# Transposed adjacency in blocks, and new order tables, in a four-layer graph network kernel

## The chip, the cores and the metric

One core of a Trainium2 chip runs the whole program in one launch. The metric is the device time of that launch in microseconds (us). The engines are TensorE (PE, with its weight loads as PEld), VectorE (DVE), ScalarE (ACT), GpSimd (POOL) and SyncE (SP, which here only issues transfers).

## What is computed

32 graphs ("batches"), each with 512 nodes of 128 features and a 512 x 512 matrix of zeros and ones in which about 3% are ones. Four residual layers, each on the row-normalised and rectified input:

```python
h = relu(layernorm(x)); x = x + L0(h)   # edge convolution: max over neighbours
#   p = h @ (W1 - W2); q = h @ W2; L0[n] = max_j relu(p[n] + q[j] + b) * adj[n, j]
h = relu(layernorm(x)); x = x + L1(h)   # 4 sublayers: adj_rownorm @ src, adj_colnorm.T @ dst, self; tanh
h = relu(layernorm(x)); x = x + L2(h)   # (adj / rowsum) @ (h @ w2) + b2
h = relu(layernorm(x)); x = x + L3(h)   # 4 steps of a gated unit (GRU) on adj.T @ (h @ w)
```

## The kernel before

**How it is staged.** `batch` (L1875) records all work of one graph: `load`, `prepare` (layer 0: layer norm, both copies of the adjacency, the neighbour lists), `gathers` (layer 0: the maximum over neighbours), `layer1`, and `layer23` (layers 2 and 3). A node takes its maximum over neighbours in two ways: up to 7 neighbours come as rows gathered by indirect transfers that POOL issues (`G<-qtab,idx`, folded in by DVE as `gm<-gm,G`), and the rest by products with one-hot matrices (`oh<-ccd` on DVE, `pa<-oh,qhl` on PE, folded in by DVE as `acc<-acc,pa`).

**Who sets the order.** Nothing is issued while it is recorded. `Flow` (L804) takes the operations of all batches and issues them one by one (`Flow.run`, `step`), engine by engine in the order of due times, which stand as text in tables: one row for each of the three weight preparations and each of the first and last batches (`FRONT`, `BACK`), and one row `MIDDLE` that is used for all batches between them, shifted by `PERIOD`. The same pass keeps a small model of engines, the port that DVE and POOL share, and the transfers; it decides ties, which PSUM bank an operation gets, and where filler matmuls (`spin`, L1077) go: they are put in front of a PE operation that the model sees start late. So the model and the tables change the program only through the order on each engine, the choice of buffers and the fillers. About four batches are under way at once: while the GRU steps of one batch run, another is in `layer1`, and two later ones are in `gathers` and `prepare`.

**The parts that matter below.**

- The transposed adjacency: four `ab` tiles (bf16 copies of 128 rows each, by ACT) go through four transposing transfers on SP into one tile `abt` (L1530 to L1532). ACT then casts it into `at`, with four operations that each read one quarter of the columns of all four transfers (L1533 to L1536). `View.meets` (L654) decides for `Flow` whether two operations touch the same part of a tile; it looks at partitions and at the second dimension of the tile alone.
- A layer norm (`norm`, L1439): DVE makes the mean and variance, then `rstd` and `shift` in small operations; POOL raises `rstd` to the power -1/2 (`rstd<-rstd,mhalf`, 128x4) and multiplies `shift` (`shift<-shift,rstd`); ACT applies both (`xn`). For layers 1 to 3 the result is split in a high part (ACT, `hi`) and a low part (POOL, `lo<-xn,hi`).
- A GRU step in `layer23`: ACT makes two gates from `pk`, POOL makes `zc = 1 - z` (`zc<-gate`), DVE multiplies `gate<-h,gate` and `nn<-nn,zc` and adds them to `h<-gate,nn`, and PE transposes `h` (`ph<-ident,h`). The transposes, and all of the next step, wait for that `h`.
- All recorded operations carry line L1051 in the profile.

Of the kernel before, what the change touches and what calls it, by code (L numbers as in the profile page):

```python
# [15 lines left out]
BF16 = mybir.dt.bfloat16  # L16
# [3 lines left out]
AF = mybir.ActivationFunctionType  # L20
# [5 lines left out]
P = 128  # L26
# [12 lines left out]
PERIOD = 80.8143  # L39
# [3 lines left out]
    380.50,  # L43
    (
        "!!!!4>!)u!,w!*U!*A!,i!3b!-/!,p!7K!Cx!Ux!f?!|6!{j!zs!{@!m&!Ac!kD##:#%##YH#[H#[S#bg#gz!ob!"
        "zw#$+#*u#eY#fJ#g:#hO#k~#o[#pD#q2#o/#ld#qT#u]#r%#rf#tq#w5#r%#n]#oE#pe#rR#p(#s3#p+#ve$$X#w"
        "G#x($#;#uc#x0$,&#z+$+F$*)#we#}S$%9$,d$*f$#x#iW#r_$.<$2A$=j$>/$C7#@0#w|#|j#}C#}U#~2#~{#x&"
        "#x.#y/#y6#yQ#z=#y=#yD#{K#{i#|[#}G#|W#}+#}=$(s$,F$.R$.H$I3$/I$CT$E!$EA$/w$1=$4)$6n$2c$=$$"
        "5K$@w$84$Am$:&$CC$>P$H{$A^$Ix$D-$No$H+$Ra$Il$T7$M)$U4$OW$[n$TC$`;$Uf$az$W,$aJ$]W$eb$`t$l"
        "&$c+$ko$ea$nT$gg$p*$l`$tk$n%$yS$oH%!S$sj$}S$u_$}j#{(#|@#~h$$%$&e#{z$*_$-&$+w$/R$#3$.3$0q"  # L50
        "$2?$4|$&&$3@$5i$6G$7c$1Q$6`$8N$;[$=v$47$<n$>b$=*$?N$6s$?W$@:$?p$A/$<C$BB$D9$C`$E$$Bb$F.$"
        "FY$Go$H>$CW$I$$Kt$LS$Ox$Eb$Nx$SV$OU$Vs$I;$Ye$]d$]l$_%$Ru$^($b2$_k$bz$V5$bb$cf$cz$dR$^D$d"
        "d$h!$fM$k2$ev$j}$l<$lc$q~$x4$yA$z!$zj%#4%$R%&s%&S%)F%(6$Jy%*5$b,%%t%>L$fe%Gk%H)%1z%47%0y"
        "%1n%0^%5I%5B%2d%8L%94%9z%:*%A9%B~%BC%AM%Aw%CW%DD%QZ%HR%Kq%M8%Pg%Q*%IW%Ip%J+%Jq%K+%L8%LO%"
        "M[%NG%JY%KB%KY%K|%L}%Ms%Qt%Rt%SC%W;%Wj%Xe%Y`%Zn%[f%[q%]B%]M%]m%^X%_8%_g%_~%`9%a9%bi%c#%d"
        "$%dO%_O%`~%b!%b:%c;%cR%cj%dS%e0%aP%dj%ee%f`%gn%iS%it%j!%j.%jL%k?%k{%lM%le%mN%r)%r@%rW%ro"
        "%sY%l6%l|%m7%m|%n7%qV%qn%s*%t:%mf%nN%oI%pD%sm%u(%v-%w<%x;%xM%xj%y&%zu%|M%}H&$i&%#&%R&&;&"
        "&j&($&(S&.{&$P&%j&&$&(<&)%&)=&)T&*&&-k&(k&/4&3M&5C&6=&7P&8z&:!&@l&BP&C_&Dv&E$&E0&E:&Ei&L"
        "r&K@&Hn&FU&M8&MF&M*&M?&N6&NN&N.&O[&RA&O~&QK&Qu&Rx&Si&_h&Y%&Yu&Z_&Zv&[<&[T&[k&^U&ct&et&fr"
        "&g+&gL&hp&kG&hU&lA&jE&kw&l[&lp&k@&l:&m:&m3&mS&mt&mL&o$&o9&oc&q.&pa&vD&w0&u(&u:&uE&uP&uo&"  # L60
        "w(&w~&xy&y5&yK&yc&yz&z5&zd&z{&{I&|H&}B&}V&~Q(!C&{M&~D&~C(!R(#?(#3($0(&2((,((7((B((M((l()"
        "Z((X()R(*M(*f(*}(+8(+O(+}(,8(,O(,{(.t(-y(0%(0a(2_(0A(26(2V(3H(45(40(5%(6`(7c(8i(8s(9Q(9p"
        "(;K(9](:V(;Q(=B(=Y(=q(>,(>C(?m(@((@R(AQ(C4(B`(Do(Ea(<$(D9(DW(E{(Fh(Fp(GX(HM(Ig(Iq(I|(J+("
        "JJ(K<(J6(K1(L,(LN(Lg(L~(M8(Mg(M~(N9(Ne(Oc(Ph(Q?(Q{(Rx(Nh(Qc(R,(Rz(Sg(S[(TW(UM(Vf(W,(W7(W"
        "X(X-(XG(Xv(Z*(ZP"
# [4 lines left out]
        1.64,  # L70
        (
            "!!!!!&!1Y!2%!1n!2E!2p!%3!4:"
# [3 lines left out]
        1.24,  # L76
        (
            "!+N!3i!4n!0#!.N!5,!4&!6]!75!6w!8]!8B!95!7O!8w!7j!9O!/9!8(!>p!?2!?R!3L!A_!Aw!@a!C{!A=!AT!"
            "AG!Aj!&7!!!!>{!BN!C$!Ck!)_!C;!CY!D0!Jb!4A!D]!E*!E]!F@!F-!F.!Fp!NO!HN!N;!NZ!,a!?=!FY!G(!G"
            "Z!H>!CY!J&!JP!K&!L2!E*!KS!K}!LS!R@!M#!M$!MP!N4!QY!O$!Y!!GT!G(!O:!OE!Q>!R8!Ra!S.!JP!RU!Rw"  # L80
            "!SJ!T+!TW!U+!K}!TL!TA!Tk!V0!WC!Wm!VQ!VR!W-!{,!Yj!~q#!q!N4!Od!XX!V~!Xd!YC!ed!]N![m!f6!k$!"
            "xR!x^!xG!yp!z]!zr!{O#.0!mW!{e!{D!{p!|f!}Q!}h!~9!~d!~O!~P!~f#$$##J##m#$0"
# [3 lines left out]
        7.83,  # L86
        (
            "!&R!(=!zB#$+##|#$6#$z#&@!!!#$Y#%)#%?#&r!,%#$e#$o#%4#(<#))#*?#()#/d#18#/o#2}#&X#0L#0)#/z#"
            "2E#32#4?#2b#=+#<|#=V#=v#0k#=6#=A#=K#?N#@;#A3#>w#F(#F`#F3#Gg#>J#F>#FI#FT#Fs#G`#I&!)(#H]#J"
            "r"  # L90
# [5 lines left out]
            "!!!!!M!!!!)I!)x!)^!)5!)q!*>!*0!*7!*X!*q!*P!,9!,M!,w!-C!-m!.D!.C!7@!:?!@N!-0!-Y!.&!.O!/&!"  # L96
            "1;!:?!@A!F/!Lo!M`!NP!Os!3T!4{!6.!Of!4#!4O!5i!:U!8#!6]!8r!9i!6]!NM!Q9!RX!Te!Qx!UE!N}!R;!X"
            "a!V%!Vc!X#!OO!R}!^i!WC!^,!]K!Pr!ZK![.!`*!_I![k!S*!SK!U=!U_!Us!V+!_?!S;!Q.!Q5!RH!R{!UJ!WR"
            "!R$!R,!R3!R:!S6!T!!RA!RO!RV!R^!Tj!V+!SR!SY!S`!Sg!Vr!X=!Y(!YH!Y>!VG!aK!iq![8!^;!f#!`O!ar!"
            "d^!c8!gF!q3!kZ!hi!j8!l}!v|!nC!q,!rN!of!~a!vY!sq!{L!u7#(=!w~##5!~T#$Z#.n#%}#(n#+p#*7#4*!Z"  # L100
            "C![>!]/![V!]s![h!]d!^_!^5!_J!Z|!]`!_.!`7!_E!a!!^|!a[!c*!cT!cA!dA!b%!cX!e-!cp!eu!bc!d+!fb"
            "!dB!gM!bx!d7!eb!h9!ey!i%!eS!g-!hV!k%!ho!kn!ic!j^!lY!k0!mF!jD!k_!n2!l1!nz!hH!ie!l`!og!m2!"
            "pR!k$!l@!mk!s3!n=!s{!qp!rl!th!s&!uS!rQ!sM!v?!se!w]!m]!q$!s{!xI!t6!{`!rA!va!x/!|K!xF!}8##"
            "=##H##S##_#4s#65#9J#7Y#9i#7y#:A!YX!]<!_P!Z9!ti!u&!rB#<V#=*#<B#<k#=W#=I#=!#=P#=j#C9#=q#DF"
            "#Q4#Ot#O##P@#Qk#S=#!Z#Qs#Q~#R]#Rg#W$#Rr#Tp#T}#U9#UF#Ux#V4#VM#Vn#T=#UR#Ul#V(#VA#VY#Vs#W!#"
            "WC#U-#Vf#W/#W;#WH#WT#Wa#Wz#Xw#U_#Wn#X*#X6#XC#Xh#Xu#Y$#YE#XO#X[#Y1#Z,#Y]#ZW#[A#[&#[S#]J#]"
            "!#]I#^*#^B#^>#^h#^b#_/#^v#_G#_S#_a#_m#`)#`N#`t#a8#_-#_y#`6#`B#`Z#`h#a##ac#b^#a1#a=#aI#aU"
            "#ao#a{#b+#bP#c##b8#bD#b]#bj#bv#c%#c3#c?#dL#cK#cW#ce#d4#d`#e2#er#e^#fn#gQ#fP#f[#h0#h;#g.#"
            "gW#hZ#i(#hF#hy#i)#iB#iZ#j0#j=#jI#k]#hS#h`#i5#iN#ih#it#jU#jb#k%#hm#j##jo#j{#k+#k7#kD#ld#m"
            "(#kP#k]#kj#l%#l2#l?#lK#lW#nI#kv#ob#lq#oo#m@#p>#ml#pj#n;#q9#ng#o6#pR#qe#r4#rt#rx#s2#sS#tK"  # L110
            "#sP#sz#u/#uX#t,#tn#t{#u+#ut#v8#vE#vQ#z6#t?#u7#uD#uP#ug#v^#vj#vw#xd#w&#w3#w@#wL#wX#we#wr#"
            "x9#|l#xE#xQ#xk#y&#y4#yK#yd#yq#{,#x_$!F#z,$!R#zW$!~#{&$#M#{R$#y#|9$$H#|f$%0#}5$%[#~3#~_$#"
            "6$&+$&V$(:$(m$(x$)%$)]$0z$2O$3k$2d$2;$2x$5[$3&$4t$5z$6@$6c$7M$9h$:4$:^$7b$;8$<=$??$<m$=p"
            "$>,$>C$>f$>}$?8$@<$@h$H4$HJ$H`$IG$J1$L!$JK$MX$L=$LP$Kk$M~$Le$Lp$NQ$NJ$Nk$PI$Nd$QV$S.$R7$"
            "Ra$Qk$VC$W/$T)$T4$T?$Ud$Wv$Xw$Yr$Zm$[($[?$[n$])$]@$]W$]o$^=$_<$`U$`J$ad$bU$^A$aP$a7$b_$c"
            "K$c?$d<$eY$fN$fY$fe$fp$g2$i$$fz$i+$jU$jm$k>$kU$km$l($lV$ln$m=$o6$n;$pD$q#$rM$p1$q+$q_$rP"
            "$s=$s1$t.$uL$vA$vd$w+$w6$wT$z<$wA$yN$zH${~$|9$|P$}!$}:$~K$~{%!I%#H%$f%$V%%u%&g$zx%&H%%D%"
            "(q%)^%)f%*Z%+^%,^%,i%,t%-!%-B%.1%-.%.)%/!%/R%/u%00%0G%0v%11%1H%1s%2r%3l%4$%4{%8:%1w%5m%4"
            "n%6{%7h%8y%9Y%:E%;:%;^%<#%</%=i%>&%<X%>~%?H"
# [3 lines left out]
        3.50,  # L123
        (
            "!!!!>B!.:!.q!.N!.%!.c!/4!/)!.j!/F!/_!/M!0l!<2!=(!<Z!?T!Mg!L6!MY!V3!]2!SU!Sv!T;!TF!Tf!PE!"
            "VD!]j!g2!pR!qC!r3!s#!U]!VB!XI!X&!Vn!Xq!YS!^c!y#!x?!zx!|X!_0!u`!v/!wN!y-!vn!yj!v<!wj!}.!x"
            "L!{m!~K!x[!yd#&u!|M#&8!}k!{Q#$8#%W#(U#)6#$w!ta!yS!~<#%u#(>#(R#4Y!a?!|O!|l!|z!}$#&T#(@!|V"
            "!|^!|e!|s!}_#![!},!}3!}9!~%#$}#%j!}m!}t!}{!~-#*T#,X#-W#;[#.W#+4#7U#99#:y#<?#=b#?(#/*#C)#"
            "4z#D[#6@#F.#8v#Gl#Co#L~#E8#N`#Fq#Qb#HN#RW#MZ#Uf#O<#WF#RK#ZU#Sn#]4#VA#_L#X0#a;#[2#d<#]m#f"
            "L#`)#hK#as#jM#eR#m]#g)#o3#i&#tS#k)#tr#n9#vD#ol#ww!~z#!v#&[##a#)+##F#%)#)s#*+#-i##*#$j#.S"  # L130
            "#/!#.l#/k#(1#)L#/&#38#/=#4##0L#1[#4l#2B#5X#2V#4z#6D#5A#70#-w#0j#5g#7y#6S#8e#2*#3E#8]#:{#"
            "8u#=%#;d#<_#=o#<v#>Z#<D#=@#?F#=W#@3#5>#:3#=}#@{#>i#Ag#=G#>c#@1#C{#@H#Dp#BG#Ef#FB#E}#G/#C"
            "=#FO#H##Fg#K3#@!#C*#F~#K|#G=#M6#D_#FL#H*#N!#O0#P6#Q*#Q5#QM#QX#xP#yo#{8#{v#|9#{V#|k#9z#2U"
            "#18#1u$&!$&=#z@#~[#~3#~p#~G$!e$#S$!l$#Z$#n$&Z$#u$(h$*?$)r$)I$(|$,P$.#$+w$*~$+X$,7$,Y$-)$"
            "-x$/V$/n$0)$0@$1A$2+$2X$3($.;$0o$1*$1p$2A$3+$3B$3Y$4)$3q$4,$5&$6h$8p$9f$:C$:N$;^$;|$<_$<"
            "m$=Y$=q$>,$>r$?D$?s$A.$AY$=($>Z$?[$@.$@[$@s$AE$A]$B:$?-$At$CA$D<$EJ$F?$Fa$Fl$Fw$G9$Gx$H*"
            "$Ik$L:$LP$N=$NS$Nk$O%$Pl$HA$J&$J=$Jl$K~$Mj$N%$OD$Ov$HX$Hp$K&$Lo$Oj$Ql$S/$T=$U2$UD$UO$Up$"
            "V2$Xu$Z-$_M$_}$`O$`g$a8$ag$bP$iN$]9$`}$aO$a~$b9$bh$c:$g)$h1$c!$dx$j,$o)$p#$q6$rH$uV$zT$|"
            "9$}G$~^%!d%!o%!z%#B%&I%)A%%T%$`%+%%+-%*t%*{%+q%,-%,0%-:%/u%/K%..%-a%0N%3x%0b%8H%9=%9T%9l"
            "%:&%:>%:U%<@%B^%D/%DD%DZ%D|%FC%I,%F(%Im%H0%IR%J2%JF%If%J+%JZ%Jf%Jy%K4%K#%LG%M)%L[%M{%MQ%"  # L140
# [2221 lines left out]
```

## Time and profile before

| what | value |
|---|---|
| median of 3 runs (lowest to highest) | 2829.79 us (2827.24 to 2830.96) |
| profiled execution, device time | 2828.67 us |
| its span, first to last instruction | 2827.0 us |
| mean granted TensorE clock | 0.991 |
| PE busy | 2723.7 us, 96% |
| DVE busy | 2432.8 us, 86% |
| POOL busy | 1730.0 us, 61% |
| ACT busy | 1268.1 us, 45% |

A busy PE is not a PE at its peak: the end of a matmul in the profile includes the time until its result stands, so two matmuls in a row overlap in the listing, and a short wait of PE can hide inside "busy". The useful number is the distance between the starts of two matmuls.

### The profile page before, as it was taken

Reading aid. Unit: us, or ns where it says so; the run is one execution under the profiler, and the core shown is the slowest. Engines: PE = TensorE matmul, PEld = TensorE weight load, DVE = VectorE, ACT = ScalarE, POOL = GpSimd, SP = SyncE. Lnnn points to the kernel's source line nnn. Section 1 sums busy time; section 2 is a strip of 40 time slices with the busy share of each in tenths; the row PEclk is TensorE's granted clock in tenths of the full one; section 3 lists DMA queues with packets and bytes.
Section 4 is the critical chain, followed back from the end, with each engine's and each line's share of the span. In section 5 each row is a group of like instructions: output and inputs, shape, how many; then the busy total and the mean of one; then the engine's idle time right before and its main releaser. Section 6 shows DMA issues by size and latency. Waiting matters only on the chain.

```text
span 2827.0 us, 36274 instructions
## 1 busy us (share of the span) xinstructions
PE 2723.7 (96%) x10703; PEld 1719.5 (61%) x10718; DVE 2432.8 (86%) x5739; ACT 1268.1 (45%) x2623; POOL 1730.0 (61%) x1892
## 2 busy tenths in 40 slices
PE   7799999999999999999999999999999999999997
PEld 3475656666666665666666666666656666556575
DVE  6888988999999998999999999999989998888543
ACT  6644444444444443444444444454444444434333
POOL 4666565666666676666667666666766666765311
PEclk9899999999999999999999999999999999999998
DMA  7754443444444443444444445444444444433100
GB/s 165 126 89 86 91 88 72 84 83 85 98 94 93 73 86 79 86 98 93 91 70 84 86 87 98 93 93 72 84 83 86 94 95 87 69 65 57 32 4 9
DMA packets 256752, 233.81 MB, mean 83 GB/s; under 512 B 98426, under 2 KB 205092, under 8 KB 256548
## 3 DMA queue, kind: packets, MB, share of 16 engines
q0 software_dynamic: 47104, 92.34, 24.3%
q1 hardware_dynamic: 143172, 81.41, 11.7%
q10 hardware_dynamic: 66272, 57.68, 6.7%
q8 instruction: 87, 1.43, 0.2%
q14 instruction: 117, 0.96, 0.1%
HBM read 163.79 MB, written 17.17 MB: 64 GB/s over the span
## 4 chain that ended last, share of the span: by engine, by line
PE 79%; DVE 10%; POOL 4%; issue 4%; ACT 3%; DMA 1%; SPq 0%; DVEq 0%; ACTq 0%; POOLq 0%
PE pg L1051 24%; PE pu L1051 18%; PE pk L1051 13%; PE pa L1051 6%; PE phn L1051 3%; PE pxn L1051 3%; PE ph L1051 2%; DVE nn L1051 2%; DVE acc L1051 2%; PE pq L1051 2%; PE pf L1051 1%; POOL G L1051 1%; PE pt L1051 1%; PE po L1051 1%; PE pkey L1051 1%
## 5 line engine op out<-in xcount | busy, mean ns | idle before, releaser
L1051 POOL DMA_INDIRECT G<-qtab,idx x744 | 829.3, 1115 | 380.6 <-DVE gm L1051 172.7
L1051 DVE TENSOR_TENSOR acc<-acc,pa 128x512 f32<-128x512 f32 x992 | 673.8, 679 | 63.3 <-PE pa L1051 30.3
L1051 PE MATMUL pa<-oh,qhl 128*128 128x512 f32 x1024 | 482.3, 497 | 15.9 <-issue 6.3
L1051 PE MATMUL pg<-an,hi 128*128 128x512 f32 (+1 forms) x1072 | 464.1, 439 | 4.4 <-ACT hi L1051 3.7
L1051 PE MATMUL pu<-ag,w 128*128 128x512 f32 (+1 forms) x952 | 443.7, 571 | 0.0
L1051 PE MATMUL pg<-an,lo 128*128 128x512 f32 (+1 forms) x1072 | 413.4, 392 | 0.0
L1051 DVE TENSOR_SCALAR oh<-ccd 128x1024 fp32r<-128x1024 bf16 x492 | 344.8, 703 | 7.1 <-DMA ccd<-cc 3.8
L1051 ACT ACTIVATE xn<-x,shift,rstd 128x128 f32<-128x128 f32 x512 | 219.3, 486 | 208.3 <-POOL shift L1051 195.0
L1051 PE MATMUL pg<-at,hi 128*128 128x512 f32 (+1 forms) x672 | 272.6, 415 | 1.1 <-ACT hi L1051 0.8
L1051 PEld LDWEIGHTS pa<-oh,qhl 128*128 128x128 f32 x1024 | 191.5, 190 | 129.3 <-issue 66.3
L1051 PE MATMUL pg<-at,lo 128*128 128x512 f32 (+1 forms) x672 | 265.3, 398 | 1.5 <-POOL lo L1051 1.3
L1051 PE MATMUL pk<-mT,g_ih 128*128 128x512 f32 (+1 forms) x528 | 252.2, 586 | 4.6 <-ACT mT L1051 4.1
L1051 PEld LDWEIGHTS pg<-an,hi 128*128 128x128 f32 x1072 | 202.1, 189 | 86.0 <-issue 36.6
L1051 ACT ACTIVATE gate<-pk,bsum 128x512 f32<-128x512 f32 (+1 forms) x264 | 171.7, 673 | 170.2 <-PE pk L1051 133.8
L1051 PE MATMUL pk<-h,g_hh 128*128 128x512 f32 (+1 forms) x528 | 245.1, 586 | 0.6 <-ACT h L1051 0.5
L1051 PEld LDWEIGHTS pu<-ag,w 128*128 128x128 f32 x952 | 172.4, 191 | 118.8 <-issue 81.9
L1051 PEld LDWEIGHTS pg<-an,lo 128*128 128x128 f32 x1072 | 201.9, 188 | 65.3 <-issue 17.5
L1051 POOL TENSOR_TENSOR rstd<-rstd,mhalf 128x4 f32<-128x4 f32 x128 | 162.4, 1269 | 114.7 <-DVE rstd L1051 89.0
L1051 DVE TENSOR_TENSOR ag<-pg,rbc 128x512 f32<-128x512 f32 (+1 forms) x272 | 172.3, 652 | 53.0 <-PE pg L1051 42.7
L1051 DVE TENSOR_TENSOR gm<-gm,G 128x128 f32<-128x128 f32 x744 | 215.1, 296 | 0.2
L1051 POOL TENSOR_TENSOR lo<-xn,hi 128x512 fp32r<-128x512 f32 x96 | 123.2, 1283 | 139.4 <-ACT hi L1051 138.6
L1051 ACT COPY mT<-pg 128x512 f32<-128x512 f32 (+1 forms) x164 | 93.7, 571 | 206.4 <-PE pg L1051 178.6
(178 smaller groups left out, 5132.2 us busy)
## 6 DMA issues: line engine op xcount, KB each, us to landing
ccd<-cc SPq DMA_DIRECT2D x512, 64.0 KB
an<-in_adj_dram POOLq DMA_DIRECT2D x128, 256.0 KB
af<-in_adj_dram ACTq DMA_DIRECT2D x31, 1024.0 KB
rbc<-scal SPq DMA_DIRECT2D x32, 512.0 KB
x<-in_x_dram ACTq DMA_DIRECT2D x62, 256.0 KB
G<-qtab,idx POOLq DMA_INDIRECT x744
qtab<-qn SPq DMA_DIRECT2D x32, 256.0 KB
out_dram<-xo ACTq DMA_DIRECT2D x32, 256.0 KB
```

What stands on the lines that cost most here:

```text
L1051: op.fn(*(real(v) for v in op.args), **{k: real(v) for k, v in op.kw.items()})
```

## The change

1. `abt` gets a fourth dimension. Transfer `it` now writes the block `abt[:, it, :, :]`, and ACT's cast reads `abt[:, :, jt, :]`, four pieces of 128 elements, and writes the same 512 elements of `at` as before. Seen by `View.meets`, the four transfers now touch different parts of the tile.
2. The model in `Flow`: a gather takes 0.55 instead of 0.35 of the shared transfer time; `idx` counts as ready 0.3 later; and a POOL operation that is not itself on the shared port (kind 1: such as `rstd`, `shift`, `g`, `dinv`) is placed behind a DVE operation that uses the port, when that one starts within `LOOK` = 0.1 after it.
3. All order tables are new. `FRONT` has 12 rows instead of 10, so that `MIDDLE` stands for 13 batches instead of 15. `PERIOD` is 80.7843 instead of 80.8143.

No other operation is added, removed or resized: the program has the same operations on every engine, apart from the filler matmuls (181 instead of 209) and the waits that follow from the order.

```diff
-PERIOD = 80.8143
+PERIOD = 80.7843
...
     HOLD = 0.6
+    LOOK = 0.1
...
         elif "pool" in at and ops["pool"].kind in (1, 2):
             at["pool"] = max(at["pool"], self.port["vec"] - self.YIELD)
+            near = self.LOOK if ops["pool"].kind == 1 else 0.0
+            if "vec" in at and ops["vec"].port and at["pool"] <= at["vec"] < at["pool"] + near:
+                at["pool"] = at["vec"] + 1e-6
...
-                self.shared = shared + (0.35 if op.after > 5.0 else 1.38)
+                self.shared = shared + (0.55 if op.after > 5.0 else 1.38)
...
-        abt = F.tile(big, [P, NT, N], BF16, tag="abt", name=f"abt_{b}")
+        abt = F.tile(big, [P, NT, NT, P], BF16, tag="abt", name=f"abt_{b}")
         for it in range(NT):
-            F.sync.dma_start_transpose(out=abt[:, :, it * P : (it + 1) * P], in_=abs_[it])
+            F.sync.dma_start_transpose(out=abt[:, it, :, :], in_=abs_[it])
         for jt in range(NT):
             F.act.activation(
-                at[:, jt, :], abt[:, jt, :], AF.Identity, accum_out=deg[:, 1, jt : jt + 1]
+                at[:, jt, :].rearrange("p (i q) -> p i q", q=P), abt[:, :, jt, :], AF.Identity,
+                accum_out=deg[:, 1, jt : jt + 1],
             )
...
             idx, at8[:, :, 0 : left(b)], float(N), none[:, :, 0 : left(b)], ALU.min, ALU.max
         )
+        F.part[-1].after += 0.3
```

The rest of the diff is the text of the tables.

## The prediction

> **What bounds the kernel now.** I read the busy time of the engines by stretches first, then the chain that ended last in order of time, then the timeline of one middle batch, and last the lists of waits. The stretches (each about one batch; columns: PE, PEld, DVE, ACT and POOL busy, clock, DMA share, GB/s):
>
> ```profile
> 302.00:383.00 81.00, 79.61 (x308) 49.63 (x307) 74.41 (x167) 36.35 (x76) 48.68 (x53) 1.00 0.44 79
> 1595.00:1676.00 81.00, 80.67 (x314) 50.66 (x311) 74.35 (x175) 36.59 (x78) 53.58 (x58) 1.00 0.48 88
> 2241.00:2322.00 81.00, 78.98 (x308) 50.10 (x307) 74.89 (x173) 37.20 (x77) 53.00 (x58) 1.00 0.42 85
> ```
>
> In the middle PE is the bound (80.67 of 81) and DVE next (74). Early and late batches leave it idle by 1.4 to 2 us more. The chain (start, length, what) repeats one piece once a batch:
>
> ```profile
> 1604.15 2.08 PE pg L1051 x9
> ...
> 1686.41 2.08 PE pg L1051 x9
> ```
>
> The period is 82.26 us, and the chain shows the same distance in nearly every middle batch. What must PE do in it? By the distance between starts in the timeline a 512-wide fp32r matmul takes 0.23 (144 a batch: `pg` 104, `pa` 32, `pc` 4, bias rows 4), a 512-wide fp32 one 0.86 (45: `pu` 21, `pk` 16, `phn` and `pxn` 8), a transpose 0.11 (49), and `pq`, `po`, `pkey` 3.5 together: 33.1 + 38.7 + 5.4 + 3.5 = 80.7 us. So about 1.6 us of each period is not matmul. Comparing each start from 1671.8 to 1754.1 with these distances, I find it in four places: `pk` after `mT` 0.28, `ph` after `h` 0.51, `pg` after `lo` 0.20, another `ph` 0.23: 1.22 together; some 0.2 more are single exposures of 0.05 between fp32 matmuls. The largest place, from the timeline (start, length, engine):
>
> ```profile
> 1685.69 0.16 DVE L1051 TENSOR_SCALAR rstd<-mv 128x4 f32<-128x4 f32 x1
> 1685.94 1.61 POOL L1051 TENSOR_TENSOR rstd<-rstd,mhalf 128x4 f32<-128x4 f32 x1 [1.99 <-DVE rstd L1051]
> 1685.96 0.69 DVE L1051 TENSOR_SCALAR oh<-ccd 128x1024 fp32r<-128x1024 bf16 x1
> ...
> 1687.63 0.20 POOL L1051 TENSOR_TENSOR shift<-shift,rstd 128x4 f32<-128x4 f32 x1
> ...
> 1691.91 1.29 POOL L1051 TENSOR_TENSOR lo<-xn,hi 128x512 fp32r<-128x512 f32 x1
> ...
> 1693.17 0.62 POOL L1051 TENSOR_SCALAR zc<-gate 128x512 f32<-128x512 f32 x1
> ...
> 1693.82 0.69 DVE L1051 TENSOR_TENSOR gate<-h,gate 128x512 f32<-128x512 f32 x1 [0.91 <-POOL zc L1051]
> ...
> 1694.73 1.03 PE L1051 MATMUL pa<-oh,qhl 128*128 128x512 f32 x2
> ...
> 1695.23 0.69 DVE L1051 TENSOR_TENSOR h<-gate,nn 128x512 f32<-128x512 f32 x1
> ...
> 1696.07 0.30 PE L1051 MATMUL ph<-ident,h 128*128 128x128 f32 x1 [0.31 <-ACT f L1051]
> ```
>
> Read it downwards. POOL's power for `rstd` starts 0.02 us before DVE's `oh` and takes 1.61. Alone it takes 1.00, and 0.61 is what was left of `oh` (1686.65 - 1685.94 = 0.71, less start-up). Everything behind it on POOL is late: `shift`, three gathers, `lo`, `zc`. DVE idles 0.91 for `zc`, its `h` lands at 1695.92, and PE, whose two `pa` had streamed out by 1695.6, starts `ph` at 1696.07. The row names `f`, which lands 0.1 later than `h`; in the program's order these transposes wait for `h` and a gate. `lo` for the next sublayer follows late on the same DVE. The hold is no rarity:
>
> ```profile
> L1051 POOL TENSOR_TENSOR rstd<-rstd,mhalf 128x4 f32<-128x4 f32 x128 | 162.4, 1269 | 114.7 <-DVE rstd L1051 89.0
> PE ph L1051 <- DVE h L1051: 25.6, 21, 2.8
> PE pw3t L1051 <- DMA w<-in_L_gnn_weight_dram: 4.2, 1, 4.2
> SPq L1051 <- DMA abt<-ab: 1.0, 1, 1.0
> ```
>
> The first row is a group of the page (busy, mean ns): 128 powers take 1.27 us on average, so 128 x 0.27 = 34 us are held. In the middle, two of the four in a period are held, always the same two, by 0.61 and 0.38 (1.38 at 1747.88). The next rows are waits (total, times, longest): `ph` for `h` is PE's largest.
>
> **The change part by part.**
>
> *Blocks of `abt`.* The last row above says that in the whole run one transfer waited 1.0 us in SP's queue for an earlier transpose. The hardware did not chain the four; only the planning did. So this part removes nothing on the chip: 0. ACT's cast `at<-abt` (0.62 us, 128 of them) now reads four pieces. If each piece cost like a 128-wide ACT operation (`xn`, 0.48), a cast would take 1.94, or 4 x 1.3 = 5.3 us more a batch on an engine with 45 us free in a period; none at the other end. I take 0, since the nearest row is the cast itself; with the cover gone it would delay `pc` and the GRU gates, which I keep as a risk of 0 to 2 us a batch. The four issues on SP (1.2 us each) stand in two pairs between the `ccd` copies instead of singly; SP is idle from 1657.8 to 1674.6 and does not bound.
>
> *Order in the middle.* In the changed program's DVE order the `rstd` that was held 0.61 is followed by `acc`, `shift`, `acc`, then `gm` and `oh`; the one that was held 0.38 by `shift`, `acc`, `acc`. `acc` reads PSUM, and the powers that ran under `acc` in this trace took 1.05. So both holds go. POOL has one more small operation in that stretch (a `shift`, 0.2). `zc` then comes about 0.4 earlier at least (0.61 - 0.2) and at most 1.0 (the first gather after `shift` lost another 0.33 against others). DVE had 0.91 of idle there, so `h` follows, and the 0.51 and the 0.20 behind it go: 0.7 a period, bounds 0.4 to 1.22. Against it, the new order has more places where PE reaches a transpose within 0.2 us of the earliest moment its `f` or `lo` can be there (7 in a period, before 2, by the work between them in PE's order and the durations of the timeline). A short wait costs about 0.1 to 0.2 with the exposed weight load (0.09 + 0.10 at 1699.50). I take one and a half new ones, 0.2, bounds 0 to 1.2. Net 0.5 x 17 batches (597 to 2001) = -8.5; bounds -20.7 (1.22 gone) to +13.6 (0.4 gone, 1.2 new).
>
> *Front and back.* In the same way I find 17 us of such waits in the batches from 165 to 597 us and 32 us in those from 2001 to 2700; nearly 20 of the 49 are `ph` for `h`, the chain shown. I take a third of the 20 as gone: -6.5; bounds -20 and +10 (half more, if the new tables carry the load worse).
>
> *Fillers.* The new program has 14 fillers in early and late batches where the old one has none. A filler costs 0 if it lies in a wait and at most 0.43 (the group's mean): 0 to +6, I take +2.
>
> *Start.* The weights that PE waited 4.2 for are issued ahead of the third batch's copies: -4.2 to 0; with other weights moved too, I take -2, bounds -8 to +5.
>
> Sum: -8.5 - 6.5 + 2 - 2 = -15 on the profiled execution's 2828.67 us: 2813.7. The median shown lies 1.1 above it: 2815.
>
> *A rule against this reading.* The power started first (1685.94 against 1685.96), yet it was the one that lost 0.61, while `oh` kept its usual 0.69. The Trainium skill, "SBUF — State Buffer", section "Who interferes with whom", says that issue order decides: whoever issues first keeps the shared ports for its whole instruction, and the other blocks. By that rule `oh` would have been held here and not POOL, moving the powers would be worth nothing to `zc`, and the sum would lose its 8.5 and half of the 6.5. I go by the row.
>
> **The rivals.**
>
> *The waits only move.* PE has 80.7 us of work in 82.26 whatever the order; each hold that goes is replaced by a hold of `g` (0.76 in this trace, a like operation takes 0.2), `dinv` (0.70 against 0.19) or a gather (1.4 against 0.95). For it: DVE is 90% busy with port users, so POOL's small operations have few free moments. Against it: `g`, `dinv` and the gathers stand ahead of more slack in this trace than the held powers do: none of the four places where PE stood still in the period follows one of them alone. Time: -15 + 8.5 + 6.5 = 0, so 2830, 2825 to 2835.
>
> *Slower: tighter PE order.* Mechanism: PE's transposes of `f` stand so close behind the last `pu` that ACT's `f` (0.69, and 0.16 until the result stands, and about 0.1 each way) ends after PE arrives. Place: the three `pf` of `layer1` and the `lo` behind them, every batch. It decides when more than about 0.7 us a batch is lost that way. At the bound above, 1.2 new against 0.4 gone: +13.6 in the middle, +2 from fillers, -2 at the start: 2843. For it: the 7 close places, and the new fillers, which show where waits are expected. Against it: in the old order such places lose only 0.1 to 0.2.
>
> *It doesn't do what it says* holds for the blocks on any branch: their direct effect is 0.
>
> **How the numbers follow.** Forecast 0.64, waits only move 0.18, slower 0.18. About 0.2% (5.7 us) is what a measurement of this kernel tells from no change. The forecast's own range is 2800 to 2826: -8.5 could be -14 or -2, -6.5 could be -12 or 0, the start 5 either way. It gives nearly all of faster; with a bit of the second case, faster 0.65. Within 0.2%: most of the second case and a little of its neighbours, 0.17. Slower: 0.18. The range, 2796 to 2838, takes in the second case and the near half of the third.
>
> **What would show it.** Right: the repeating piece of the chain comes every 81.5 to 81.9 us; the mean of POOL's `rstd` group falls from 1269 to 1100 ns or less; DVE's idle before `gate<-h,gate` shrinks, and PE's wait for `h` falls below 20. The `at<-abt` cast stays at 0.62. Wrong: the mean of `rstd` falls and the period stays (then the chain through `zc` was not what PE waited for), or PE waits for ACT `f` grow by 10 us or more, or the cast gets longer.

## The result, and the profile after

| | median | lowest to highest | runs |
|---|---|---|---|
| before | 2829.12 us | 2824.26 to 2830.96 | 6 |
| after | 2814.89 us | 2811.83 to 2817.08 | 6 |

The ratio is 0.9952, with a 95% interval from 0.9939 to 0.9964: 14 us faster. The profiled execution after took 2811.83 us, with a span of 2810.1, 16.9 us shorter than the span before.

The same stretches as before, by engine (columns: PE, PEld, DVE, ACT and POOL busy, clock, DMA share, GB/s), then the repeating piece in the chain that ended last (start, length, what):

```profile
302.00:383.00 81.00, 79.32 (x304) 48.95 (x302) 74.53 (x174) 34.16 (x69) 48.99 (x53) 1.00 0.43 79
1595.00:1676.00 81.00, 80.73 (x313) 51.18 (x311) 75.62 (x176) 37.23 (x78) 52.48 (x58) 1.00 0.46 88
2241.00:2322.00 81.00, 79.16 (x305) 48.63 (x304) 73.27 (x175) 37.45 (x80) 54.61 (x59) 1.00 0.47 88
```

```profile
1597.97 1.85 PE pg L1107 x8
...
1679.97 1.85 PE pg L1107 x8
```

PE is the bound as before, and the period of the middle is now 82.0 (81.95 to 82.0 in most batches) instead of 82.26. The kinds of lines that the prediction rested on, first the group and then the waits (total, times, longest):

```profile
L1107 POOL TENSOR_TENSOR rstd<-rstd,mhalf 128x4 f32<-128x4 f32 x128 | 139.9, 1093 | 102.1 <-DVE shift L1107 50.4
```

```profile
PE ph L1107 <- DVE h L1107: 22.3, 43, 2.4
DVE gate L1107 <- POOL zc L1107: 35.3, 30, 5.0
PEld pa L1107 <- DVE acc L1107: 23.0, 39, 1.2
```

The power takes 1.09 us on average instead of 1.27, and DVE waits 35 us for `zc` instead of 67. But PE's wait for `h` only fell from 25.6 to 22.3, and the wait of `pa`'s weight loads for `acc` doubled (11.5 before).

Where did the 16.9 us of the two profiles come from? The distance between output transfers cuts both executions at the same points of the work:

| stretch | before | after | difference |
|---|---|---|---|
| start to first output | 288.0 | 280.3 | -7.7 |
| first to sixth output | 419.0 | 421.5 | +2.5 |
| sixth to 22nd output (the middle) | 1321.9 | 1318.4 | -3.6 |
| 22nd output to the end | 798.0 | 790.0 | -8.1 |

The first of these rows varies between executions of one and the same order: four of the kernels below have the start of the kernel before, and their first output came at 285.3, 288.2, 291.4 and 291.4; three have the start of the changed kernel, without touching it, and there it came at 281.9, 284.8 and 285.8. With the two rows of the table the means are 288.9 and 283.2. The other stretches repeat within some 2 us where the order in them is the same, apart from the new order's end: in five executions it took 790.0 to 797.0, in six of the old order 797.5 to 799.8.

In a steady period the waits of PE, from the distances between starts as in the prediction, are these (us, places that wait over 0.06):

| | before (1589.5 to 1671.8) | after (1578.8 to 1660.8) |
|---|---|---|
| `pk` for `mT` | 0.18 + 0.10 | none |
| `ph` for `h` | 0.48 + 0.18 | 0.33 + 0.07 |
| `pg` behind `lo` | 0.10 + 0.10 | none |
| `pa` for `acc`, and `pg` behind it | none | 0.42 + 0.11 |
| sum | 1.14 | 0.93 |

So the old places are clear, but for 0.07 of `ph`, and most of that has come in again at new ones: 1.07 gone, 0.86 new (the 0.33 is at the `h` of another step). This is the piece around the power that was held 0.61, with all of POOL's operations in the stretch (timeline after: start, length, engine):

```profile
1597.07 0.16 DVE L1107 TENSOR_SCALAR rstd<-mv 128x4 f32<-128x4 f32 x1
1597.14 0.68 DVE L1107 TENSOR_TENSOR acc<-acc,pa 128x512 f32<-128x512 f32 x1
1597.32 1.05 POOL L1107 TENSOR_TENSOR rstd<-rstd,mhalf 128x4 f32<-128x4 f32 x1 [0.21 <-DVE rstd L1107]
1597.85 0.69 DVE L1107 TENSOR_TENSOR acc<-acc,pa 128x512 f32<-128x512 f32 x1
1598.44 0.20 POOL L1107 TENSOR_TENSOR shift<-shift,rstd 128x4 f32<-128x4 f32 x1
...
1602.92 1.29 POOL L1107 TENSOR_TENSOR lo<-xn,hi 128x512 fp32r<-128x512 f32 x1
1604.16 0.63 POOL L1107 TENSOR_SCALAR zc<-gate 128x512 f32<-128x512 f32 x1
1604.82 0.69 DVE L1107 TENSOR_TENSOR gate<-h,gate 128x512 f32<-128x512 f32 x1 [0.58 <-POOL zc L1107]
```

The power runs under two `acc` and takes 1.05; DVE waits 0.58 for `zc` where it waited 0.91. And this is the largest new wait of a period:

```profile
1581.62 0.68 DVE L1107 TENSOR_SCALAR oh<-ccd 128x1024 fp32r<-128x1024 bf16 x1
1581.75 1.68 POOL L1107 TENSOR_TENSOR lo<-xn,hi 128x512 fp32r<-128x512 f32 x1 [0.42 <-issue]
...
1582.22 1.36 DVE L1107 TENSOR_TENSOR gm<-gm,G 128x128 f32<-128x128 f32 x1
...
1583.50 0.68 DVE L1107 TENSOR_SCALAR oh<-ccd 128x1024 fp32r<-128x1024 bf16 x1
...
1584.10 1.46 DVE L1107 TENSOR_TENSOR acc<-acc,pa 128x512 f32<-128x512 f32 x2
...
1584.83 0.50 PE L1107 MATMUL pa<-oh,qhl 128*128 128x512 f32 x1 [0.27 <-DVE acc L1107]
```

Here it is DVE that is held. POOL's `lo` starts 0.13 behind an `oh` and takes 1.68 instead of some 1.28, so it lost 0.4 to it; then it keeps what it got, and `gm`, which takes 0.28 elsewhere, takes 1.36. `oh` and `acc` are late by 1.1, and PE's `pa` waits for the `acc`.

### The profile page after: what moved, and what is told of

The parts are those of the page before. It is cut to its first block, busy times and chain, and to the rows that moved or that the text cites. A ratio compares the mean times of both kernels' runs of the same rounds, so it can differ in the third digit from the quotient of the medians.

```text
span 2810.1 us, 36215 instructions
## 1 busy us (share of the span) xinstructions
PE 2715.8 (97%) x10690; PEld 1719.9 (61%) x10690; DVE 2450.8 (87%) x5739; ACT 1263.9 (45%) x2623; POOL 1687.4 (60%) x1892
## 4 chain that ended last, share of the span: by engine, by line
PE 62%; DVE 21%; issue 7%; ACT 4%; POOL 4%; DMA 2%; SPq 0%; ACTq 0%; DVEq 0%; POOLq 0%
PE pg L1107 19%; PE pu L1107 13%; PE pk L1107 11%; DVE acc L1107 5%; PE pa L1107 4%; PE phn L1107 3%; DVE nn L1107 3%; PE pxn L1107 2%; DVE oh L1107 2%; DVE gm L1107 2%; PE ph L1107 2%; DVE h L1107 2%; ACT xn L1107 2%; DVE gate L1107 2%; PE pq L1107 1%
## 5 line engine op out<-in xcount | busy, mean ns | idle before, releaser
L1107 POOL DMA_INDIRECT G<-qtab,idx x744 | 786.5, 1057 | 530.3 <-DVE gm L1107 324.8
L1107 PE MATMUL pa<-oh,qhl 128*128 128x512 f32 x1024 | 469.5, 488 | 18.6 <-DVE acc L1107 8.4
L1107 PE MATMUL pg<-an,hi 128*128 128x512 f32 (+1 forms) x1072 | 453.0, 429 | 0.2 <-ACT hi L1107 0.2
L1107 PE MATMUL pg<-at,hi 128*128 128x512 f32 (+1 forms) x672 | 284.1, 432 | 2.6 <-ACT hi L1107 1.9
L1107 PE MATMUL pk<-h,g_hh 128*128 128x512 f32 (+1 forms) x528 | 251.3, 582 | 0.9 <-ACT h L1107 0.7
L1107 DVE TENSOR_TENSOR gm<-gm,G 128x128 f32<-128x128 f32 x744 | 232.8, 328 | 7.5 <-DMA G<-qtab,idx 6.5
L1107 POOL TENSOR_TENSOR lo<-xn,hi 128x512 fp32r<-128x512 f32 x96 | 130.9, 1363 | 120.7 <-ACT hi L1107 116.4
L1107 POOL TENSOR_TENSOR rstd<-rstd,mhalf 128x4 f32<-128x4 f32 x128 | 139.9, 1093 | 102.1 <-DVE shift L1107 50.4
```

What stands on the lines that cost most here:

```text
L1107: op.fn(*(real(v) for v in op.args), **{k: real(v) for k, v in op.kw.items()})
```

## The experiments

Each run was measured beside fresh runs of the kernel before, whose medians were 2828.8 to 2830.3; the ratio is to those.

Most edits move due times inside the row `MIDDLE`, so they act in the middle batches alone (15 of the kernel before, 13 of the changed one). `row[k]` is the due time of the k-th operation of a batch, and `old` the row as it was. The order on the engines is that of the kernel named, but for what the edit moves.

| run | from | median | ratio to before, 95% interval | middle period |
|---|---|---|---|---|
| e1 | before | 2829.53 | 1.0004 (0.9994 to 1.0013) | 82.26 |
| e2 | before | 2828.38 | 1.0000 (0.9990 to 1.0011) | 81.72 or 82.26 |
| e5 | before | 2824.57 | 0.9977 (0.9967 to 0.9986) | 81.97 |
| e9 | before | 2827.76 | 0.9996 (0.9987 to 1.0006) | 82.15 |
| e7 | before | 2833.35 | 1.0009 (1.0000 to 1.0019) | 82.26 |
| e3 | after | 2825.94 | 0.9992 (0.9981 to 1.0002) | 82.71 |
| e4 | after | 2808.57 | 0.9929 (0.9913 to 0.9946) | 81.32 |
| e6 | after | 2812.21 | 0.9931 (0.9914 to 0.9947) | 81.35 |
| e8 | after | 2817.46 | 0.9954 (0.9937 to 0.9970) | 81.96 |
| e10 | after | 2800.83 | 0.9904 (0.9887 to 0.9920) | 81.29 |
| e11 | after | 2811.15 | 0.9931 (0.9914 to 0.9947) | 81.62 |

**e1: all of the change except the tables.** The kernel before, with the blocks of `abt` and the planner's new numbers.

```diff
+    LOOK = 0.1
...
-                self.shared = shared + (0.35 if op.after > 5.0 else 1.38)
+                self.shared = shared + (0.55 if op.after > 5.0 else 1.38)
...
-            F.sync.dma_start_transpose(out=abt[:, :, it * P : (it + 1) * P], in_=abs_[it])
+            F.sync.dma_start_transpose(out=abt[:, it, :, :], in_=abs_[it])
...
+        F.part[-1].after += 0.3
```

> The kernel before with everything of the change except the tables: the blocks of abt, and the new numbers of the planner. The order on DVE, ACT, POOL and SP, and of PE's work without fillers, is that of the kernel before. Theory (the gain is in the order alone): 2829, within 5 us; abt's cast stays at 0.62 us for 512 columns; period 82.26. Rival (the blocks themselves free the transfers or speed the cast): 2825 or less. Other rival (four pieces make the cast dear): cast above 0.7 us, 2835 or more.

Measured: no change, the period 82.26, the cast 0.62 (from the list of the tile's operations: lowest, median and highest ns):

```profile
L1055 ACT ACTIVATE at<-abt x128: 613/619/643, 34.0 to 2490.6; 128x512 fp32r<-128x512 bf16 x128
```

Both rivals fall: four pieces of 128 cost what one row of 512 cost, and the transfers gain nothing. What the blocks allow is an order: in four of the 32 batches the new tables issue two of the four transfers in another order than they are recorded, which the old layout would have forbidden.

**e2: the hold taken out of the old order.** One `oh` goes behind two `acc`.

```diff
+        row[215] = old[223] + 0.0
+        row[217] = old[215] + 0.0
+        row[223] = old[132] - 0.004
```

> The kernel before, in the 15 middle batches with one oh behind two acc instead of ahead of them, so that the power which was held 0.61 us runs beside acc. Theory (the held power delays shift, lo, zc and h): rstd there 1.05 instead of 1.61; zc 0.5 earlier or more; the wait of ph that was 0.5 a period and the pg wait of 0.2 behind it go; period 81.6 to 81.9 instead of 82.26, time 2819 to 2824. Rival (the waits only move): rstd 1.05, period 82.2 to 82.3, time 2829.

Measured: every one of the edited powers took 1.04, and the median did not move. The profiled execution was one of the two fastest of ten (2819.7; eight took 2826 to 2830), and it has both kinds of batch in it. Two of its batches, from the power to `ph`:

```profile
1183.97 1.04 POOL L1059 TENSOR_TENSOR rstd<-rstd,mhalf 128x4 f32<-128x4 f32 x1 [1.97 <-DVE rstd L1059]
...
1187.19 0.75 DVE L1059 TENSOR_SCALAR oh<-ccd 128x1024 fp32r<-128x1024 bf16 x1
1187.21 0.95 POOL L1059 DMA_INDIRECT G<-qtab,idx  x1 [0.30 <-issue]
...
1190.69 0.62 POOL L1059 TENSOR_SCALAR zc<-gate 128x512 f32<-128x512 f32 x1
1191.34 0.69 DVE L1059 TENSOR_TENSOR gate<-h,gate 128x512 f32<-128x512 f32 x1 [0.38 <-POOL zc L1059]
...
1265.73 1.04 POOL L1059 TENSOR_TENSOR rstd<-rstd,mhalf 128x4 f32<-128x4 f32 x1 [1.99 <-DVE rstd L1059]
...
1268.93 0.68 DVE L1059 TENSOR_SCALAR oh<-ccd 128x1024 fp32r<-128x1024 bf16 x1
1268.97 1.46 POOL L1059 DMA_INDIRECT G<-qtab,idx  x1 [0.30 <-issue]
...
1272.95 0.62 POOL L1059 TENSOR_SCALAR zc<-gate 128x512 f32<-128x512 f32 x1
1273.61 0.69 DVE L1059 TENSOR_TENSOR gate<-h,gate 128x512 f32<-128x512 f32 x1 [0.91 <-POOL zc L1059]
```

In both the power is free. Then a gather meets the next `oh`: in the first batch it starts 0.02 behind it and takes 0.95, and `oh` takes 0.75; in the second it starts 0.04 behind it and takes 1.46. From there all is 0.51 later, `zc`, `gate` and `ph`, and DVE waits the same 0.91 for `zc` as in the kernel before. The first batch takes 81.7 and the second 82.3. So the hold had only moved, from the power to the gather.

The trace has this piece in 14 of the 15 edited batches, and they agree without exception: in eight the gather starts 25 to 33 ns behind `oh` and takes 0.95, in six it starts 35 to 39 ns behind it and takes 1.46 or 1.47. `zc` starts 6.7 behind the power in the eight and 7.2 in the six. What shifts the start by those few ns is not shown.

**e5: and the gather freed.** As e2, and the `oh` that meets the gather goes ahead of the `ag` before it.

```diff
+        row[228] -= 0.606
```

> As the run with the power's hold taken out of the kernel before, and besides one oh is moved ahead of the ag before it, out of the way of the gather that started within 0.05 us of it and in some batches lost 0.5 us to it. In the profile of that run every power took 1.04, yet the period was 81.7 in half of the middle batches and 82.25 in the others, and the two kinds differ first in this gather (0.95 or 1.46). Theory (the hold on POOL moves from the power to the gather, and zc, h and ph follow whichever is there): gather 0.95 in all of them, period 81.7 in all 15 middle batches, time 2819 to 2823. Rival (something else decides between the two kinds): period still mixed or 82.25, time 2827 to 2829.

Measured: 5.7 us faster than before, and the mixture is gone: the period is 81.94 to 82.0, but for four batches that are longer in the kernel before too. `ph` waits 0.18 instead of 0.48. The size fell between the two expectations: the gather ahead of that one now meets the moved `oh` and takes 1.35 instead of 1.12.

```profile
1521.90 1.35 POOL L1060 DMA_INDIRECT G<-qtab,idx  x1 [0.49 <-DVE acc L1060]
...
1527.69 0.69 DVE L1060 TENSOR_TENSOR gate<-h,gate 128x512 f32<-128x512 f32 x1 [0.63 <-POOL zc L1060]
```

The theory holds, with the 0.23 that is left put down to that gather. Two `oh` moved in the old order give the new order's period, although the second held power of each period still takes 1.38 here: that hold costs nothing that shows.

**e3: the hold put back into the new order.** One `oh` ahead of the two `acc`.

```diff
+        row[223] = old[215] - 0.004
```

> The changed kernel, in the 13 middle batches with one oh moved up to stand right behind the shift and rstd of DVE, so that it meets the power again. Theory: rstd there 1.6 instead of 1.05, zc and h 0.5 later, period 82.2 to 82.5 instead of 81.95, time 2819 to 2823. Rival (h in the new order has slack, so the hold costs nothing): rstd 1.6, period 81.95, time 2815.

Measured: the period is 82.71, 0.75 more, and the median 11 us above the changed kernel's. The timeline, to be laid beside that of after:

```profile
1605.64 0.69 DVE L1113 TENSOR_SCALAR oh<-ccd 128x1024 fp32r<-128x1024 bf16 x1
1605.81 1.42 POOL L1113 TENSOR_TENSOR rstd<-rstd,mhalf 128x4 f32<-128x4 f32 x1 [0.21 <-DVE rstd L1113]
...
1607.96 0.69 DVE L1113 TENSOR_SCALAR oh<-ccd 128x1024 fp32r<-128x1024 bf16 x1
1608.12 1.43 POOL L1113 DMA_INDIRECT G<-qtab,idx  x1 [0.62 <-DVE gm L1113]
...
1614.06 0.69 DVE L1113 TENSOR_TENSOR gate<-h,gate 128x512 f32<-128x512 f32 x1 [1.32 <-POOL zc L1113]
...
1616.23 0.30 PE L1113 MATMUL ph<-ident,h 128*128 128x128 f32 x1 [0.65 <-DVE h L1113]
```

The power loses 0.37 and the gather behind it, which took 1.16, another 0.27. DVE waits 1.32 for `zc` instead of 0.58, 0.74 more, and this is what the period grew by. The theory was right on the mechanism and too low on the size, because it counted the power alone.

**e9: `zc` earlier without freeing anything.** In the old order `zc` goes ahead of `lo` on POOL.

```diff
+        row[574] -= 1.24
```

> The kernel before, with one POOL operation moved in the 15 middle batches: the zc of the waiting GRU step goes ahead of lo instead of behind it. The held power, the held gather and all of DVE's order stay. In the runs so far, ph moved with the end of this zc one to one (0.24 or 0.53 earlier, or 0.74 later). Theory (what counts is when POOL comes to zc, by whatever way): zc about 1.2 earlier, the ph wait of 0.48 gone, period 81.7 to 81.8, time 2820 to 2823, though the powers still take 1.61. Rival (lo, now 0.6 later, is needed as soon): period 82.2 or more, 2828 or more.

Measured: `zc` came 1.16 earlier, the period only fell by 0.11, and the median within the noise. What became of the 1.16:

```profile
1606.66 0.62 POOL L1057 TENSOR_SCALAR zc<-gate 128x512 f32<-128x512 f32 x1
1607.26 1.27 POOL L1057 TENSOR_TENSOR lo<-xn,hi 128x512 fp32r<-128x512 f32 x1
1607.49 1.58 DVE L1057 TENSOR_TENSOR gate<-h,gate 128x512 f32<-128x512 f32 x1
...
1609.80 0.68 DVE L1057 TENSOR_TENSOR h<-gate,nn 128x512 f32<-128x512 f32 x1
```

DVE's `gate` starts at once, 0.23 behind POOL's `lo`, and is held by it: 1.58 instead of 0.69. The theory's "by whatever way" is wrong: here an earlier `zc` is worth little, because the `gate` that follows runs into the next long POOL operation. The rival is near in the numbers, but its reason, that `lo` is needed as soon, is not what these rows show.

**e7: the start.** The weight transfer that PE waited 4.2 us for, earlier on SP.

```diff
+    front[2][2] = 78.0
```

> The kernel before with the one weight transfer for which PE waited 4.2 issued some ten transfers earlier on SP. Theory (the start gains by this alone): that wait falls under 1, everything behind is 2 to 5 us earlier, time 2824 to 2827. Rival (the transfers that it is put ahead of are what the next products wait for): wait gone, time 2827 to 2831.

Measured: the 4.2 us wait is gone from the list of waits, and the first output came at 293.8, later than in any execution with the old start; the median is 3 us above before, higher than either expectation. Other things are then waited for, as the rival says (waits of PE's `pa`, this run and then before; nearly all that is new lies in the first 300 us):

```profile
PE pa L1053 <- DVE oh L1053: 10.4, 4, 6.6
PE pa L1053 <- DVE acc L1053: 8.3, 7, 4.6
PE pa L1051 <- DVE oh L1051: 1.4, 1, 1.4
PE pa L1051 <- DVE acc L1051: 2.2, 4, 1.0
```

The planner also put 16 more fillers in, so the 3 us are not the transfer's alone. But moved by itself this transfer gives no earlier start.

**e8: fillers.** The changed kernel without the 23 fillers between 150 and 2650 us.

```diff
-        if self.spin and gap > self.IDLE and n > 0:
+        if self.spin and gap > self.IDLE and n > 0 and not 150.0 < t < 2650.0:
```

> The changed kernel without the 23 fillers between 150 and 2650 us of the plan; those of the start and the end stay. Theory (a filler lies in a wait or costs up to 0.43): 2808 to 2815, at most 6 us faster and no slower; granted clock at 440 to 520 and 2180 to 2290 us still 1.00. Rival (they keep the clock up): the clock falls to 0.5 there for some us, time 2816 or more.

Measured: 0.9954 of before where the changed kernel had 0.9952, so the fillers cost nothing that can be measured. (The median, 2817.46, lies above the expected range; the runs of before beside it were 1.1 higher than those in the table of the result.) The clock stays at 1.00 at 440 to 520 and at 2180 to 2290 without them. At 178 to 192 us, where 9 of the 23 were, it fell to 0.77 (1.00 in the changed kernel), though not at a place that the rival named:

```profile
178.00:192.00 14.00, 9.87 (x34) 6.18 (x33) 13.68 (x40) 6.89 (x14) 10.55 (x11) 0.77 0.29 64
440.00:520.00 80.00, 76.60 (x292) 47.69 (x291) 69.08 (x162) 34.95 (x73) 50.74 (x56) 1.00 0.42 85
2180.00:2290.00 110.00, 103.92 (x395) 64.35 (x395) 95.47 (x215) 47.22 (x99) 72.76 (x77) 1.00 0.43 86
```

**e4: the new wait cleared.** In the changed kernel two `acc` go ahead of the `gm` and `oh` that POOL's `lo` holds.

```diff
+        row[197] = old[120] + 0.0
+        row[200] = old[120] + 0.6
+        row[120] = old[200] + 0.004
+        row[208] = old[200] + 0.008
```

> The changed kernel; its largest new wait is pa, 0.42 a period, for an acc that stands behind a gm which took 1.36 instead of 0.28 while POOL's lo ran. Here two acc stand ahead of that gm and of the oh behind it. Theory (DVE is held by lo there, and PE waits for the acc): gm 0.3, the pa wait gone, period 81.4 to 81.6, time 2808 to 2811. Rival (ph for h is next at once, or the gathers behind gm come late): period 81.9 to 82.0, time 2815.

Measured: 2808.57, the period 81.32, 0.63 less. The `pa` wait is gone, and the wait of `ph` went from 0.33 to 0.21. The timeline:

```profile
1580.11 0.68 DVE L1116 TENSOR_SCALAR oh<-ccd 128x1024 fp32r<-128x1024 bf16 x1
1580.24 1.68 POOL L1116 TENSOR_TENSOR lo<-xn,hi 128x512 fp32r<-128x512 f32 x1 [0.42 <-issue]
1580.71 0.67 DVE L1116 TENSOR_TENSOR acc<-acc,pa 128x512 f32<-128x512 f32 x1
...
1582.54 0.28 DVE L1116 TENSOR_TENSOR gm<-gm,G 128x128 f32<-128x128 f32 x1
...
1584.28 1.39 POOL L1116 TENSOR_TENSOR rstd<-rstd,mhalf 128x4 f32<-128x4 f32 x1
```

`lo` still takes 1.68, but DVE has `acc` to do, which is not held, and `gm` is back at 0.28. The last row is a power that took 1.05 in the changed kernel: the moved work holds it again in every middle batch, and the period falls all the same. The intervals of the two times touch (0.9913 to 0.9946 here, 0.9939 to 0.9964 for the changed kernel), so it is the period that shows the gain.

**e10: the same in the rows around the middle.** The same four lines in ten more batches, five ahead and five behind.

> The changed kernel with gm and oh behind two acc, as in the run that took its period to 81.32, now in ten more batches: the five ahead of the middle ones and the five behind, whose rows have the same order there. Theory (each such batch loses the same 0.5 to 0.6 to POOL's lo): 3 to 6 us less than with the middle ones alone, 2803 to 2807. Rival (those batches wait for other things): 2808 to 2812.

Measured: 2800.83, better than expected, 28 us below before and 14 below the changed kernel; the interval ends at 0.9920, below the changed kernel's 0.9939. In its profile the sixth to 22nd output take 1305.1, 13.3 less than after, and 14 of the 17 periods in and next to the middle take 81.25 to 81.32. It beats both kernels, with a mean power of 1149 ns where the changed kernel has 1093.

**e6 and e11: what is left of `ph`.** e6 is e4 with `zc` ahead of one gather and one `st` behind an `nn`; e11 is e10 with both and with the `acc` ahead of `nn` put behind it (the third line, in e11 alone).

```diff
+        row[410] += 0.2
+        row[544] -= 0.951
+        row[210] += 2.0
```

> The changed kernel with gm and oh behind two acc (which took its period from 81.95 to 81.32), and besides zc ahead of one gather on POOL and one st behind nn on DVE, in front of the ph that still waits 0.33 a period. Theory (h's own chain through zc and the two small delays on DVE sets that wait): period 80.9 to 81.1, time 2803 to 2806. Rival (the gather behind zc and the gm behind it come late, or PE waits next for something else): 81.2 to 81.4, 2808.

> As the run before it, and in the 13 middle batches the chain of one h is cleared: one acc and one st go behind the two nn on DVE, and zc goes ahead of one gather on POOL. With zc and st alone ph did not move, because nn stood behind acc on DVE. Theory (the acc in front of nn is the rest of that ph's wait, 0.21): ph there 0 to 0.05, period 81.1, 2 to 4 us less than the run before it. Rival (the acc, now later, keeps a bank of PSUM and PE waits for that): period 81.3 or more, same time or longer.

Measured: in e6 `zc` came 0.8 earlier and `ph` still waits 0.2 to 0.26, since `nn` ends no sooner. In e11 `nn` starts 0.28 earlier, but the `acc` now stands ahead of `gate`, which starts 0.37 later, and `ph` waits 0.63. Both rivals have the period right; of their reasons, late gathers and a kept PSUM bank, neither is what these rows show. DVE has no free time between the two `nn` and `h`; moving work within that piece only changes which of its operations is late. e6 and e4 cannot be told apart by their intervals.

## Why the prediction was right

The forecast was 2815 and the median is 2814.89. That is closer than its steps deserve: the middle gained less than half of its term and the start nearly three times its own, and these misses nearly cancel. To this extent the hit is luck. That the gain is in the order is shown by e1; why the order helps is shown for the middle only, which is 3.6 of the 16.9 us between the profiles.

**Blocks, 0: right**, shown by e1.

**The held powers: right as a mechanism.** The two powers that were held take 1.05, and the mean fell to 1093 ns, where 1100 or less was named. Only the one that lost 0.61 counts: the other is held at 1.38 in e5 and again at 1.39 in e4 and e10, all three with a shorter period than the kernels that they were made from. So the mean of the power is no sign of the time. That a hold on POOL reaches PE nearly one to one through `zc`, `gate` and `h`, where these follow at once, is shown from both sides: put back, it cost 0.74 in DVE's wait for `zc` and 0.75 of period (e3); taken out of the old order together with the gather's, it gave 0.29 of period for a `zc` 0.30 earlier (e5). e9 is the limit: there `gate` met a new hold. The freed power alone gave nothing in the median (e2), which the prediction did not see: it named gathers in the rival "the waits only move", but took the power as the hold that decides.

**The middle, -8.5: mis-sized.** The term was 0.7 gone less 0.2 new, times 17. Gone are 1.07, for `pk` and most of the other `ph` went too; new are 0.86, not 0.2. The step that failed is "I take one and a half new ones, 0.2". The bound of 1.2 held it. (The 0.33 of a first gather, in the upper bound for `zc`, stands in no row: the three gathers there take 1.03, 1.00 and 0.94.) It looked for new waits only where PE comes close behind an `f` or a `lo` of its own operands, with the other engines' durations as they were; the largest new one, 0.42 for `acc`, comes from DVE being held by POOL, a hold in the other direction, which the prediction did not look for (e4 shows it and takes it away). The period fell by 0.3, which would be some 4.6 in 16 batches; a few batches that are longer in both kernels, around 1100 and 1400 us, took 1.0 more after, so the sixth to 22nd output gained 3.6. Why those are longer was not looked into.

**The start, -2: too small.** By means over executions it gained about 5.7 (288.9 to 283.2). The weights issued early do not give it by themselves (e7). The traces show that PE stands still less: up to the first output it has no matmul but fillers for 80 to 89 us in five executions of the old start, and for 73 to 77 in four of the new. Which change of the order does this stays open.

**Front and back, -6.5: near as a sum (-5.6 between the two profiles), wrong in its parts.** The first to sixth output lost 2.5, and the end gained 8.1: the gap before the last output fell from 50.4 to 38.3, and other batches of the end gave some of that back. After the 31st output 149 matmuls are left to PE instead of 180, so work of the last batch stands earlier, and PE's time with no matmul but fillers from the 22nd output on fell from 52.9 to 43.5. The term took `ph` for `h` as what would go; PE's wait for it fell by 3.3 in the whole run. I read this in the profiles and made no experiment on it. The end also varied by 7 us between runs of the new order; by the means over executions that have the old or the new end it gained 5.7 and the front lost 3.1, a sum of -2.6.

**Fillers, +2: nothing** (e8).

**The rivals.** "The waits only move" is largely true for the middle: 0.86 came in for 1.07 gone, though by none of the holds that it named. It is also what e2 (here a gather, as named), e9 and e11 did. One argument for it was wrong: DVE's 90% are not all port users, since `acc`, which the powers run beside unheld, is 21 of the 82 us of a period. "Slower", by PE waiting for `f`, did not come: PE's waits of `pf` for `f` went from 3.0 to 4.1 in the whole run, and those of `ph` that the profile puts down to `f` from 5.3 to less than 1. The cast stayed at 0.62.

**What would show it**, as named: the power's mean and the cast came as said; the piece comes every 82.0 and not 81.5 to 81.9; PE's wait for `h` is 22.3 and not under 20. Both misses say the same as the middle term: less net gain there. The sign that it gave for being wrong, that the power falls and the period stays, nearly came.

The rule weighed in the prediction, that of the Trainium skill's "SBUF — State Buffer", section "Who interferes with whom", that issue order decides who blocks, does not describe these rows if order is read from recorded starts: in e2 the gather starts 25 to 33 ns behind `oh` and is not held, and 35 to 39 ns behind it and is held. That the one which has the port keeps it for its whole instruction agrees with `gm` at 1.36 and `gate` at 1.58.

## What to carry to other kernels

When two engines hold each other, look at the holds in both directions and at every operation behind the one you free: a hold that is taken from one operation can be paid by the next (e2, e9). A hold costs only where something waits for it at once: the powers of e4 and e10 are held again, and these are the fastest kernels here. Count what an order adds as carefully as what it removes: list the places where a long operation of one engine lies beside a port user of the other, and put work there that does not use the port (`acc`, which reads PSUM: four due times in e4 and e10, 14 us below the changed kernel). A forecast that hits the total can still have its terms wrong, so compare it stretch by stretch.

## What was not expected of the hardware

- A difference of some 10 ns in the recorded start of a POOL operation, against DVE's `oh`, goes with a difference of 0.5 us in what it takes, and it fell both ways in one execution (e2: 25 to 33 ns and 0.95, 35 to 39 ns and 1.46). An order that depends on it has two times.
- Between executions of one order the first 290 us vary by 6 us, while the steady period repeats to 0.05.
- A POOL operation of 1.28 us that was waiting for an `oh` goes ahead of DVE's next operation, although the start of that one is recorded at once: DVE then loses 1.1 us to it (`gm` 1.36 after, 0.28 in e4).
